# Attention and a mixture of experts on one Trainium2 core: the last sums loaded first, stored from another queue and shared with GpSimd; one batch's choice a call later; four fillers of each head behind a group of transposes

## The chip, the cores and the metric

The kernel runs on one core of a Trainium2 chip, in one launch. A core has a matrix engine (TensorE; in the profile PE, its weight loads PEld), VectorE (DVE), ScalarE (ACT) and GpSimd (POOL), each with an instruction stream of its own, and SyncE (SP), which here only issues transfers. Transfers run on 16 DMA engines; each issuing engine has a queue. Work is held in SBUF (128 partitions), matmul results in PSUM, which has eight banks of 128 x 512 float32.

The metric is the device time of the launch in microseconds (us). The kernel before took 1003.43 us, the median of three runs (1003.37 to 1006.6).

## The reference

2048 tokens of width E = 128, float32 throughout. Causal attention with H = 16 heads of D = 64, a residual, then a mixture of 8 experts (two of them per token, hidden width F = 352) beside a shared expert, and a residual:

```python
x = x + attention(layernorm(x))          # qkv with bias, causal softmax(q k / 8) v, out projection with bias
z = layernorm(x)
shared = (silu(z @ sg.T) * (z @ su.T)) @ sd.T
probs = softmax(z @ gate_w.T)             # 8 experts
topw, topi = top_k(probs, 2);  topw = topw / (topw.sum(-1) + 1e-20)
for e in 8 experts:                       # comb[t, e]: weight of expert e for token t, 0 where not chosen
    routed += (silu(z @ gw[e].T) * (z @ uw[e].T)) @ dw[e].T * comb[:, e]
x = x + shared + routed
```

## The kernel before, in words

**Attention.** Heads are handled in eight pairs j = 0..7 ("head" below means a pair; one takes about 100 us). A head runs through eight steps, each a pair m of token blocks of 128 (256 queries), in the order `turns = [2, 7, 0, 6, 1, 5, 3, 4]` (L393). Per step: scores of q and k (`score_units`, L438, `sc` in PSUM), scaled, masked and with their row maxima on VectorE (L449, L453), exponentials on ScalarE (L470), the probabilities turned, multiplied with v (`times_v`, L570, `av`), divided by their sums (`divide`, L591, the tile `aT`, of which there is one) and projected back to width 128 (`project`, L597, `po`), which is added to the residual `xr` (L598). So a probability row must be turned between exponential and value product. For m below 4 TensorE does it: `turn` (L538) transposes into a PSUM tile `tr` and ScalarE copies that to a tile `pT` (L541). For m of 4 and above ("near" in the code) the leading part is turned by VectorE's 32 x 32 transposes and a trip through device memory (`turn_slabs` stores to `staged`, `load_turned` loads it back as `turned`); only the last two or four blocks are turned by TensorE, by `turn_last`, which copies them to the tile `tail`.

**Fillers.** While head j runs, the queries, keys and values of head j + 1 are made by twelve short units: `qk_unit` (L361: one matmul of 128 x 512 into `pq`; keys are then copied by ScalarE at L373, queries by VectorE) and `v_unit` (L378: four matmuls into `pv`, copied by ScalarE at L385). They stand in the queue `fill`, one taken per group of a step. In the loop over steps and groups (L681 to L758) a step whose m is below 4 takes its filler at the start of a group, ahead of the group's transposes (L715 to L717), and a near step after the value products, ahead of `turn_last` of the step two later (L739 to L748).

**Order.** TensorE and VectorE work in the order in which the code writes their instructions (L630). ScalarE's and GpSimd's instructions are ordered by a scheduler. Six PSUM banks go round under the tag "r" for `sc`, `tr`, `pq`, `pv`, `po` and the rest; two hold `av`. A new tile takes the place of the one that was given out longest ago, so a matmul that writes `sc` may wait for the copy that empties a `tr`.

**Choice of experts.** When a pair of steps in the last head is finished, `route_units` makes the choice of experts for its four token blocks: normalised rows, their transposes, logits (`pr`, L260), the best expert (`best1`, six small VectorE operations and an exponential), the second best (`best2`), ranks by a matmul with a triangular matrix (`rk`, L301), then scatters of the rows to `zbuf` (L328). It returns a list of units, `None` meaning that a call does nothing; `route_on` (called up to three times in a group) takes the next one. For batches 0 and 1 the list is statistics, normed, None, turn, None, logits, None, best1, best2, None, None, ranks.

**Experts.** Rows come back sorted by expert in 39 blocks of 128, each goes through gate, up and down products, and GpSimd scatters the result to `ybuf` (L991). Each token has two rows there. The shared expert is done in four groups of 512 tokens; the group `late` (2) comes after all the experts' blocks, and its result `py` is added to `xr` at L811.

**End.** A loop over the four groups of 512 tokens in order 0, 1, 2, 3 loads the group's two rows per token (`yt`, 0.52 MB, L1026, on SyncE's queue), adds them to `xr` with two VectorE operations (L1028), and stores the group (L1031, on SyncE's queue too). As the scheduler put it before, SyncE issues three loads, the store of group 0, the fourth load and the other stores.

Of the kernel before, what the change touches and what calls it, by code (L numbers as in the profile page):

```python
# [10 lines left out]
F32 = mybir.dt.float32  # L11
# [5 lines left out]
P = 128  # L17
# [6 lines left out]
def attention_then_moe(  # L24
# [32 lines left out]
    nc = tc.nc  # L57

    _, S, E = x.shape
# [5 lines left out]
    NG = NT // 4  # L65
# [5 lines left out]
    out2 = out.rearrange("b (t p) e -> p (b t) e", p=P)  # L71
# [6 lines left out]
    xr = const.tile([P, NT, E], F32, name="xr")  # L78
# [4 lines left out]
    def load_wq(j, engine):  # L83
        wq_of[j] = norm.tile([P, 3, 2, D], F32, tag="wq", name=f"wq_{j}", bufs=3)
        engine.dma_start(wq_of[j], qkv_w[:, :, 2 * j : 2 * j + 2, :])
# [7 lines left out]
    with nc.allow_non_contiguous_dma(reason="1024 numbers"):  # L93
# [16 lines left out]
        fill=MASKED,  # L110
# [6 lines left out]
    for e in range(NE):  # L117
# [9 lines left out]
        fill=0.0,  # L127
# [86 lines left out]
    def route_units(blocks, number):  # L214
        n, k0 = len(blocks), blocks[0]
# [119 lines left out]

        turns = [lambda t0=t0: turn_row(t0) for t0 in range(0, n, 4)]
        chosen = [logits, None, best1, best2, ranks]
        if number < 2:
            chosen[4:4] = [None, None]
        if number == len(batches) - 1:  # L340
            return [statistics, normed, *turns, logits, best1, best2, ranks]
# [12 lines left out]
    def qkv_units(j):  # L354
        kT = pool.tile([P, S], F32, tag="kT", name=f"kT_{j}")
        qT = [None] * NG
        vt = pool.tile([P, NT, P], F32, tag="vt", name=f"vt_{j}")

        def qk_unit(s, n):
            pq = psp.tile([P, 512], F32, tag="r", name=f"pq_{j}_{s}_{n}")  # L360
            nc.tensor.matmul(  # L361
                pq,
                wq_of[j][:, s, :, :],
                xnT[:, ts(n, 512)],
                start=True,
                stop=True,
            )
            bias = bqk[:, s, j : j + 1]
            if s == 0:
                qT[n] = pool.tile([P, 512], F32, tag=f"qT{n}", name=f"qT_{j}_{n}", bufs=1)  # L370
                nc.vector.tensor_scalar_add(qT[n], pq, bias)  # L371
            else:
                nc.scalar.activation(kT[:, ts(n, 512)], pq, AF.Identity, bias=bias)  # L373

        def v_unit(g):
            pv = psp.tile([P, 4, P], F32, tag="r", name=f"pv_{j}_{g}")
            for t in range(4):
                nc.tensor.matmul(  # L378
                    pv[:, t, :],
                    xnT[:, ts(4 * g + t, P)],  # L380
                    wq_of[j][:, 2, :, :],
                    start=True,
                    stop=True,
                )
            nc.scalar.copy(vt[:, ts(g, 4), :], pv)  # L385

        q, k = ([lambda s=s, n=n: qk_unit(s, n) for n in range(NG)] for s in range(2))
        return (kT, qT, vt), q, k, [lambda g=g: v_unit(g) for g in range(NG)]
# [10 lines left out]
    def by_slabs(m):  # L399

        return (2 * m) // 4 * 4 if 2 * m >= NT // 2 else 0
# [130 lines left out]
    def turn(j, m, b, dst):  # L532

        tr = psp.tile([P, 2, 256], F32, tag="r", name=f"tr_{j}_{m}_{b}")
        q0 = 1 if b == 2 * m + 1 else 0
        for h in range(2):
            for q in range(q0, 2):
                nc.tensor.transpose(  # L538
                    tr[:, h, ts(q, P)], rows_of[j, m][q][:, h, ts(b, P)], ident
                )  # L540
        nc.scalar.copy(dst[:, :, q0 * P :], tr[:, :, q0 * P :])  # L541

    def turn_last(j, m):

        tail_of[j, m] = pool.tile([P, 4, 2, 256], F32, tag="tail", name=f"tail_{j}_{m}", bufs=1)
        for b in range(by_slabs(m), 2 * m + 2):
            turn(j, m, b, tail_of[j, m][:, b - by_slabs(m)])
# [41 lines left out]
    def divide(j, m):  # L589
        aT = pool.tile([P, 256], F32, tag="aT", name=f"aT_{j}_{m}", bufs=1)  # L590
        nc.vector.tensor_mul(aT, av_of[j, m], inb_of[j, m])  # L591
        return aT
# [28 lines left out]
    steps = [(j, m) for j in range(NP) for m in turns]  # L621
    qkv = {0: qkv_units(0)}

    def scores_of(n):
        if n >= len(steps):
            return deque()
        j, m = steps[n]
        return deque(score_units(j, m, *qkv[j][0][:2]))
# [14 lines left out]
    fill, later = deque(), deque()  # L643
# [20 lines left out]
    def route_on():  # L664

        for units in routes:
            u = units.popleft()
            if u:
                u()
        routes[:] = [units for units in routes if units]  # L670
# [10 lines left out]
    for n, (j, m) in enumerate(steps):  # L681
        at = n % NM
        if at == 0 and j + 1 < NP:
            qkv[j + 1] = qkv_units(j + 1)


            _, q, k, v = qkv[j + 1]
            fill.extend([*k, *v, q[3]])
            later.extend([q[1], q[0], q[2]])
            if j + 2 < NP:  # L690
                load_wq(j + 2, nc.sync)
        if at == 0 and j == NP - 1:
            load_shared()
        if at == 5 and later:
            assert not fill
            fill.extend(later)
            later.clear()
        if at == 6 and j + 1 < NP:
            assert not fill
        near = by_slabs(m)  # L700
        coming = scores_of(n + (4 if near else 2))
        if n == 0:
            coming.extend(scores_of(3))

        if near:
            groups = [list(range(near, 2 * m + 2))]
            groups += [list(range(k, k + near // 2)) for k in range(0, near, near // 2)]

            runs = [3, 3, len(coming) - 6] if n > 1 else [0, 3, 3]
        else:  # L710
            groups = [list(range(k, min(k + 3, 2 * m + 2))) for k in range(0, 2 * m + 2, 3)]
            half = len(coming) // 2 if n else 6
            runs = {1: [len(coming)], 2: [2 * (half // 2), half], 3: [0, half, half]}[len(groups)]
        for k, group in enumerate(groups):
            for _ in range(1 if n else 3):  # L715
                if fill and not near:
                    fill.popleft()()  # L717
            if n == 2:
                turn_slabs(2, age=False)
            turn_slabs(1)  # L720
            now = [turned(j, m, b) for b in group]
            if k == 0:
                spread(j, m)
            if ending is not None:
                finish(*ending)
                ending = None
            if n >= len(steps) - 2 and (n < len(steps) - 1 or k < 2):
                route_on()
            ready, last = (last + now, []) if near else (last, now)
            for t in ready:  # L730
                jt, mt, b = t[:3]
                times_v(*t, qkv[jt][0][2])
                if b == (by_slabs(mt) or 2 * mt + 2) - 1:
                    assert ending is None
                    ending = (jt, mt, divide(jt, mt))
            if n < len(steps) - 2:
                route_on()

            for _ in range(1 if n > 1 or k == 2 else 2):  # L739
                if fill and near:  # L740
                    fill.popleft()()
            if n < 2 and k == 1 - n:
                turn_slabs(2, age=False)
            turn_slabs(1, age=False, due=True)
            if n >= len(steps) - 2:
                route_on()
            if near and k == 0 and n + 2 < len(steps):
                turn_last(*steps[n + 2])  # L748
            if n == 0 and k == 0:
                turn_last(*steps[1])  # L750
                load_turned(*steps[1])
            if near and k == 1 and n + 2 < len(steps):
                load_turned(*steps[n + 2])
            for _ in range(runs[k] if k < len(groups) - 1 else len(coming)):
                if coming:
                    coming.popleft()()
            if len(steps) - 4 <= n < len(steps) - 2:
                route_on()  # L758
# [8 lines left out]
    ffn = ctx.enter_context(tc.tile_pool(name="ffn", bufs=2, reuse_waits="tile"))  # L767
# [47 lines left out]
    late = turns[-1] // 2  # L815
# [25 lines left out]
    number, started, which, mine, left, real = (tabs[:, k, :] for k in range(6))  # L841
# [179 lines left out]


    yb = ybuf.rearrange("(t p s) e -> p t (s e)", p=P, s=2)
    for g in range(NG):
        yt = ffn.tile([P, 4, 2 * E], F32, tag="yt", name=f"yt_{g}", bufs=NG)
        nc.sync.dma_start(yt, yb[:, ts(g, 4), :])  # L1026
        for k in range(2):
            nc.vector.tensor_add(  # L1028
                xr[:, ts(g, 4), :], xr[:, ts(g, 4), :], yt[:, :, k * E : (k + 1) * E]
            )  # L1030
        nc.sync.dma_start(out2[:, ts(g, 4), :], xr[:, ts(g, 4), :])  # L1031


# [53 lines left out]
```

## Time and profile before

| What | us |
|---|---|
| median of three runs | 1003.43 (1003.37 to 1006.6) |
| the profiled execution's own time | 1008.16 |
| its span, first to last instruction | 1006.30 |
| TensorE busy (share of the span) | 943.7 (94%) |
| VectorE busy | 749.7 (75%) |
| ScalarE busy | 540.9 (54%) |
| GpSimd busy | 204.9 (20%) |
| scores L438, TensorE | 298.0 in 1280 matmuls, mean 552 ns |
| value products L570, TensorE | 237.9 in 1920 matmuls |
| transposes L538, TensorE | 121.4 in 896 |
| fillers L361, TensorE | 71.3 in 128 |
| exponentials L470, ScalarE | 306.2 in 256 |
| scatters L991, GpSimd | 38.3 in 39 |

The span is what the trace shows; the execution's own time has 1.86 us more around it. The profile is of one execution, and the times are of others. Busy time is time in which an engine runs an instruction; its idle time is put down to the instruction that ended it. Where the prediction shows a line such as `431.66 0.83 ACT L541 COPY tail<-tr ... x2`, the columns are the start in us, the length of the stretch in us, the engine, the line of the code, the operation, the tile written and the tiles read, the shapes, and how many instructions of the kind follow on each other; in square brackets stands the idle time just ahead and what ended it. "PEclk" is the clock that TensorE was granted, 1.00 being full speed. An issue of a transfer is listed under its queue (SPq for SyncE's).

### The profile page before, as it was taken

What the parts mean: (1) busy time and instruction counts of PE and PEld (TensorE: products, weight loads), DVE (VectorE), ACT (ScalarE), POOL (GpSimd) and SP (SyncE); (2) the same over time, 40 slices, a digit from 0 to 9 for tenths busy, and PEclk for the clock granted to TensorE, in tenths of its full rate; (3) what the DMA queues carried; (4) which work ended last, traced back from release to release, by engine and by line L of the source; (5) the groups of instructions that cost most, each with busy time, mean ns of one, the idle gap of its engine ahead of it and who ended that gap; (6) DMA issues with size and microseconds to landing.
All of it is one profiled execution on the core that took longest, in us unless ns stands there. A gap on an engine that the chain in (4) does not pass through costs nothing. (4 is left out here: it accounts for less than half of the span.)

```text
span 1006.3 us, 18409 instructions
## 1 busy us (share of the span) xinstructions
PE 943.7 (94%) x5930; PEld 567.9 (56%) x5930; DVE 749.7 (75%) x2359; ACT 540.9 (54%) x1017; POOL 204.9 (20%) x393
## 2 busy tenths in 40 slices
PE   4998899999999999999999999999999898989996
PEld 1464555565556555655565556555655455657774
DVE  3786788778877877787778777877788886755554
ACT  4573556555655565556555655565466553425552
POOL 2040111111111111111111111111211103634441
PEclk9998999999999999999999999999999997999998
DMA  9568648864896488748874887588648864723104
GB/s 329 173 203 288 198 149 267 261 220 155 261 276 206 155 260 265 216 157 261 270 210 157 260 266 210 164 256 270 209 150 274 268 193 146 216 61 85 40 24 132
DMA packets 112670, 205.31 MB, mean 204 GB/s; under 512 B 16864, under 2 KB 104258, under 8 KB 107456
## 3 DMA queue, kind: packets, MB, share of 16 engines
q1 hardware_dynamic: 102816, 190.65, 59.4%
q0 software_dynamic: 8032, 13.22, 5.5%
q8 instruction: 48, 0.79, 0.3%
q10 hardware_dynamic: 1728, 0.27, 0.2%
q14 instruction: 46, 0.38, 0.1%
HBM read 105.10 MB, written 99.35 MB: 203 GB/s over the span
## 5 line engine op out<-in xcount | busy, mean ns | idle before, releaser
L470 ACT ACTIVATE row<-row,neg 128x1920 f32<-128x1920 f32 (+15 forms) x256 | 306.2, 1202 | 198.7 <-DVE neg L467 87.3
L438 PE MATMUL sc<-kT,qT 64*128 64x512 f32 (+3 forms) x1280 | 298.0, 552 | 11.3 <-ACT tail L541 5.2
L449 DVE TENSOR_SCALAR_CACHE_REDUCE row<-sc 128x512 f32<-128x512 f32 x384 | 243.3, 685 | 76.4 <-PE sc L438 65.8
L438 PEld LDWEIGHTS sc<-kT,qT 64*128 64x128 f32 x1280 | 123.9, 186 | 152.5 <-issue 83.6
L512 DVE STREAM_TRANSPOSE row<-row 128x1024 f32<-128x1024 f32 (+1 forms) x128 | 190.3, 1491 | 5.1 <-ACT row L470 5.1
L570 PE MATMUL av<-turned,vt 128*64 128x256 f32 x1280 | 158.3, 395 | 2.1 <-DMA turned<-stage 2.1
L453 DVE CUSTOM_DVE_ANT_0 row<-sc,mask 128x384 f32<-128x384 f32 (+3 forms) x256 | 114.9, 486 | 18.2 <-PE sc L438 17.6
L538 PE MATMUL tr<-ident,row 128*128 128x128 f32 x896 | 121.4, 281 | 6.5 <-DVE row L449 2.1
L538 PEld LDWEIGHTS tr<-ident,row 128*128 128x128 f32 x896 | 102.2, 144 | 41.1 <-issue 19.4
L570 PEld LDWEIGHTS av<-turned,vt 128*64 128x64 f32 x1280 | 88.5, 140 | 64.9 <-issue 23.5
L501 POOL DMA_DIRECT2D invd<-inv x60 | 43.1, 718 | 392.1 <-DVE inv L499 285.1
L541 ACT COPY pT<-tr 128x512 f32<-128x512 f32 (+1 forms) x160 | 78.6, 553 | 77.6 <-PE tr L538 77.2
L583 POOL DMA_DIRECT2D inb<-invd x120 | 71.6, 602 | 187.8 <-DMA invd<-inv 112.7
L570 PE MATMUL av<-pT,vt 128*64 128x256 f32 (+1 forms) x640 | 79.6, 371 | 6.3 <-ACT pT L541 5.9
L361 PE MATMUL pq<-xnT,wq 128*128 128x512 f32 x128 | 71.3, 647 | 0.1
L570 PEld LDWEIGHTS av<-pT,vt 128*64 128x64 f32 x640 | 38.5, 136 | 46.9 <-ACT pT L541 18.8
L541 ACT COPY tail<-tr 128x512 f32<-128x512 f32 x96 | 43.9, 520 | 15.1 <-PE tr L538 15.1
L991 POOL DMA_INDIRECT ybuf<-yo,to x39 | 38.3, 982 | 61.3 <-ACT yo L990 61.3
L371 DVE TENSOR_SCALAR qT<-pq,bqk 128x512 f32<-128x512 f32 x32 | 23.9, 747 | 34.6 <-PE pq L361 34.6
L470 ACT ACTIVATION_READ_ACCUMULATOR row<-row,neg 128x1 f32 x256 | 49.6, 194 | 0.0
L597 PE MATMUL po<-wo,aT 128*128 128x128 f32 x256 | 43.7, 294 | 5.7 <-DVE rest L280 2.5
L597 PEld LDWEIGHTS po<-wo,aT 128*128 128x128 f32 x256 | 34.0, 193 | 22.9 <-DVE row L449 16.3
(170 smaller groups left out, 894.8 us busy)
## 6 DMA issues: line engine op xcount, KB each, us to landing
stage<-row SPq DMA_DIRECT2D x256, 192.0 KB, 3.7
turned<-stage SPq DMA_DIRECT2D x16, 3072.0 KB, 11.1
stage<-row SPq DMA_DIRECT2D x256, 128.0 KB, 2.7
turned<-stage SPq DMA_DIRECT2D x16, 2048.0 KB, 8.7
zbuf<-zeros SPq DMA_DIRECT2D x8, 1056.0 KB, 11.4
inb<-invd POOLq DMA_DIRECT2D x120, 64.0 KB, 3.2
zs<-zbuf SPq DMA_DIRECT2D x39, 66.0 KB, 1.8
yt<-ybuf SPq DMA_DIRECT2D x4, 512.0 KB, 4.2
```

Source lines behind the costliest of these rows:

```text
L361: nc.tensor.matmul(pq, wq_of[j][:, s, :, :], xnT[:, ts(n, 512)], start=True, stop=True,)
L438: nc.tensor.matmul(sc[:, :cw], qT[i // 4][hd, ts(i % 4, P)], keys, start=True, stop=True)
L449: nc.vector.tensor_scalar(dst, src, SCALE, None, ALU.mult, ALU.max, accum_out=mh)
L453: nc.vector.tensor_tensor_reduce(out=rows[:, h, c0 : c0 + cw], in0=scs[h][:, :cw], in1=mask[:, 512 - cw : 512], scale=SCALE, scalar=-F32_M ...
L470: nc.scalar.activation(row, row, AF.Exp, bias=neg[:, h : h + 1], accum_out=sums[:, h : h + 1])
L501: small_dma(j, m)(invd_of[j, m].rearrange("n (a i) -> a n i", a=4), inv,)
L512: nc.vector.transpose(row, row)
L538: nc.tensor.transpose(tr[:, h, ts(q, P)], rows_of[j, m][q][:, h, ts(b, P)], ident)
L541: nc.scalar.copy(dst[:, :, q0 * P :], tr[:, :, q0 * P :])
L570: nc.tensor.matmul(av_of[j, m][hd, q0 * P :], vt[:, b, hd], pT[:, h], start=(b == near), stop=(b == (near or 2 * m + 2) - 1),)
L583: small_dma(j, m)(inb[h * D : (h + 1) * D, :].rearrange("d (q p) -> d q p", q=2), row.partition_broadcast(D),)
L597: nc.tensor.matmul(po[:, q, :], aT[:, ts(q, P)], wo[:, j, :], start=True, stop=True)
```

## The change

Three parts, and nothing is computed differently.

1. **Fillers and `turn_last`.** In the first step of a head (m = 2, two groups; not in the very first step of the run) the second group takes its filler behind the group's transposes and ahead of the value products, where it took it ahead of the transposes. In near steps, `turn_last` of the step two later comes ahead of the first group's filler, where it came behind it (for all steps but the run's second, where it stays). Other steps are as they were.
2. **Choice of the first batch.** One more None ahead of `best1` and one fewer behind `best2`: `best1` and `best2` come one call later, and ranks at the same call. The second batch keeps its list.
3. **End.** All four loads are written ahead of the sums, in the order 0, 1, 3, 2; the second of them, group 1, is added by GpSimd; the stores go out on ScalarE's queue.

```diff
         chosen = [logits, None, best1, best2, ranks]
-        if number < 2:
+        if number == 0:
+            chosen = [logits, None, None, best1, best2, None, ranks]
+        if number == 1:
             chosen[4:4] = [None, None]
...
             for _ in range(1 if n else 3):
-                if fill and not near:
+
+                if fill and not near and (at or not k or not n):
                     fill.popleft()()
...
             if n >= len(steps) - 2 and (n < len(steps) - 1 or k < 2):
                 route_on()
+            if n and not at and k and fill:
+                fill.popleft()()
             ready, last = (last + now, []) if near else (last, now)
...
             if n < len(steps) - 2:
                 route_on()
+            if n > 1 and near and k == 0 and n + 2 < len(steps):
+                turn_last(*steps[n + 2])
 
             for _ in range(1 if n > 1 or k == 2 else 2):
                 if fill and near:
...
-            if near and k == 0 and n + 2 < len(steps):
+            if n == 1 and k == 0:
                 turn_last(*steps[n + 2])
...
     yb = ybuf.rearrange("(t p s) e -> p t (s e)", p=P, s=2)
-    for g in range(NG):
-        yt = ffn.tile([P, 4, 2 * E], F32, tag="yt", name=f"yt_{g}", bufs=NG)
-        nc.sync.dma_start(yt, yb[:, ts(g, 4), :])
+    by_group = [g for g in range(NG) if g != late] + [late]
+    yts = {}
+    for g in by_group:
+        yts[g] = ffn.tile([P, 4, 2 * E], F32, tag="yt", name=f"yt_{g}", bufs=NG)
+        nc.sync.dma_start(yts[g], yb[:, ts(g, 4), :])
+    for g in by_group:
+        engine = nc.gpsimd if g == by_group[1] else nc.vector
         for k in range(2):
-            nc.vector.tensor_add(
-                xr[:, ts(g, 4), :], xr[:, ts(g, 4), :], yt[:, :, k * E : (k + 1) * E]
+            engine.tensor_add(
+                xr[:, ts(g, 4), :], xr[:, ts(g, 4), :], yts[g][:, :, k * E : (k + 1) * E]
             )
-        nc.sync.dma_start(out2[:, ts(g, 4), :], xr[:, ts(g, 4), :])
+        nc.scalar.dma_start(out2[:, ts(g, 4), :], xr[:, ts(g, 4), :])
```

How this falls out in the instruction streams: TensorE's and VectorE's are as written, ScalarE's copies follow their matmuls. In heads 1 to 6 four fillers per head end up behind a group of transposes: the second keys unit in m = 2, the third keys unit in m = 7, a values unit in m = 6 and a queries unit in m = 5; in head 0 only the one in m = 5. There, in heads 1 to 6, the first copy of the tail of m = 4 also comes ahead of the exponentials of m = 7 on ScalarE, where it stood behind them. The streams of SyncE and GpSimd are the same up to the end; there SyncE issues four loads in a row and ScalarE, behind all its other work, the four stores in the order 0, 1, 3, 2.

## The prediction

> **What bounds the kernel now.** I read the busy times by stretch first, then TensorE's order of time over one head, then ScalarE and VectorE at the same instants, and last the queues of the end.
>
> ```profile
> core 0: us, PE busy (x) PEld busy (x) DVE busy (x) ACT busy (x) POOL busy (x), PEclk, DMA share, GB/s
> 270.00:390.00 120.00, 116.87 (x769) 67.58 (x769) 94.91 (x279) 71.21 (x130) 20.21 (x40) 1.00 0.74 223
> ...
> 820.00:832.20 12.20, 9.94 (x70) 6.05 (x68) 11.51 (x43) 8.05 (x19) 0.00 (x0) 1.00 0.58 142
> 832.20:845.90 13.70, 12.91 (x57) 8.91 (x58) 7.60 (x47) 2.72 (x8) 2.99 (x3) 0.50 0.60 206
> ```
>
> In the middle of the run TensorE is busy 97% of the time; VectorE has a fifth free, ScalarE two fifths. So time can only be won from TensorE's gaps. They recur with each head, 100.24 us apart (the wait at 332.04 us in head 2 comes again at 432.27 in head 3). Around 832 us the granted clock is 0.50 for 13.7 us; I come back to that.
>
> ```profile
> 427.36 1.13 PE L361 MATMUL pq<-xnT,wq 128*128 128x512 f32 x2
> 428.32 0.82 PE L538 MATMUL tr<-ident,row 128*128 128x128 f32 x6
> 429.07 2.59 PE L438 MATMUL sc<-kT,qT 64*128 64x512 f32 x8
> 432.27 1.40 PE L438 MATMUL sc<-kT,qT 64*128 64x512 f32 x4 [0.62 <-ACT tail L541]
> 433.60 0.71 PE L597 MATMUL po<-wo,aT 128*128 128x128 f32 x4
> ```
>
> ```profile
> 429.38 1.15 ACT L470 ACTIVATE row<-row,neg 128x1024 f32<-128x1024 f32 x1 [3.02 <-DVE neg L467]
> ...
> 431.57 0.18 ACT L470 ACTIVATION_READ_ACCUMULATOR row<-row,neg 128x1 f32 x1
> 431.66 0.83 ACT L541 COPY tail<-tr 128x512 f32<-128x512 f32 x2
> ```
>
> This is the largest gap that a moved filler stands at. The filler pq comes ahead of the transposes tr, so tr ends only at 429.1; ScalarE, idle for 3.02 us until 429.38, then has two exponentials first and copies tr out of PSUM at 431.66. The scores sc need those PSUM tiles: 12 matmuls from 429.07 to 433.60 are 4.53 us, where the undisturbed group at 389.55 takes 2.78.
>
> ```profile
> 829.38 1.06 PE L260 MATMUL pr<-gwT,xnT 128*128 128x8 f32 x8
> 832.99 1.19 PE L597 MATMUL po<-wo,aT 128*128 128x128 f32 x4 [2.55 <-DVE rest L280]
> 834.11 3.68 PE L570 MATMUL av<-turned,vt 128*64 128x256 f32 x16
> ```
>
> The projection po waits 2.55 us, really for aT, which VectorE makes at 832.44 behind six small operations of the first batch's choice (831.27 to 832.44).
>
> ```profile
> 991.47 1.49 SPq L1026 DMA_DIRECT2D yt<-ybuf  x3
> 996.73 0.38 SPq L1031 DMA_DIRECT2D out_dram<-xr  x1
> 997.15 0.51 SPq L1026 DMA_DIRECT2D yt<-ybuf  x1
> 998.58 4.57 SPq L1031 DMA_DIRECT2D out_dram<-xr  x3
> ```
>
> ```profile
> 997.87 2.02 DVE L1028 TENSOR_TENSOR xr<-xr,yt 128x512 f32<-128x512 f32 x3
> 1001.33 1.42 DVE L1028 TENSOR_TENSOR xr<-xr,yt 128x512 f32<-128x512 f32 x2 [1.45 <-DMA yt<-ybuf]
> ```
>
> The fourth load stands behind a store that waits for sums, so it starts 5.7 us after the first and the last sums end at 1002.75.
>
> **Fillers and turn_last.** Nothing is added: the same matmuls and copies in another order, no DMA among them; SyncE's and GpSimd's queues keep their order here. Per head four fillers move from ahead of a group of transposes to behind it.
> (a) First key/query filler of step m=2. In head 3, tr comes 0.86 us earlier (pq takes 372.23 to 373.09), but the next av waits for a copy that ScalarE makes at 375.28, after two exponentials of 1.80 and 1.79 us. The filler was before that wait and is still before it, so the 0.98 us wait at 375.91 stays. Only the copy of pq (0.71 us) no longer stands ahead of three pT copies; the score pair at 377.31 took 0.78 us against 0.53 for the same pair at 413.96. I take 0.1, with 0 and 0.25 as bounds.
> (b) Filler of m=7: no gap there. Behind tr, its kT copy (0.69 us) comes last and would be done at about 383.45; the score that reuses its tile begins at 384.4. Nothing, with 0.9 us of cover.
> (c) Filler of m=6 (four value products): the copy comes after four tail copies (1.84 us from about 404.0), done at about 406.5; its user begins at 407.35. Nothing, cover 0.85 us.
> (d) Filler of m=5, the gap shown: tr ends at about 428.1, ScalarE is idle, and in the changed order the first tail copy is ahead of the exponentials. Left behind them is the second, of 128x256 (0.38 us, row at 360.00): 431.66 + 0.38 = 432.04. Only the last score product waits for it: two passes, 0.53 + 0.43, to 433.06 instead of 433.60. That is 0.54. Bounds: 0 if another copy takes the place, 1.75 (4.53 - 2.78) if the wait vanished.
> In head 0 ScalarE's order is unchanged; I give it nothing. Heads 1 to 6: 6 x 0.64 = 3.8 us. It stays won if nothing later holds absolute time: the next loads of turned rows land well ahead (issued 410.64, median 11.1 us to landing, used 434.24), and VectorE waits for TensorE at 437.28 (1.91 us).
>
> **First batch's choice.** Six VectorE operations, 1.09 us, go from ahead of aT to behind it. po starts 1.1 us sooner. Next, rk waits for the choice itself, which ends when it did (834.3). At full clock TensorE reaches rk at 834.4, so no wait; then it reaches the second batch's rk earlier, and that waits for a VectorE chain which stays where it was: VectorE works without a break from 822 to 836.5. So at full clock 0.2 of the 1.1 is left; at half clock, where VectorE idles 3.57 us at 840.07, the whole 1.1. Bounds 0 and 1.1.
> The row with the half clock: 16 av matmuls take 3.61 us at 834.11 and 1.88 at 434.24. From po to the second rk (832.99 to 846.50) half rate costs about 6.3 us, some 5.5 after the VectorE chain. The Trainium skill (TensorE: Matmul & The Clock Gate, HAM oscillation) says that idle gaps over some 3.4 us throttle the array. Here the gap was 2.55 us and the clock fell all the same, so the row decides; by the rule no throttle stood here to be lost.
>
> **End.** All four loads issue from 991.47, 0.55 apart. The engines moved 382 GB/s while three loads were queued (993.5 to 997.0), so 2.10 MB from about 993.2 end at 998.7; with the first group's store (0.26 MB, issued about 996.8) mixed in, 999.4. VectorE: group 0 to 996.65, py to 997.95, group 3 to 999.2, the late group from 999.5 to 1000.9, against 1002.75: 1.85 us. GpSimd adds group 1. The trace has no 128x512 add on it: 128x128 takes 0.45 (paced 0.415), memsets grow from 0.19 to 0.53 for the same step in size. Between 1.2 and 1.8 each; I take 1.5, the add being the nearer row, so 996.5 + 3.0 = 999.5, before the late group. It stands behind the last scatter (ended 990.32), and nothing is behind it but group 3's and the late group's stores, which follow group 1's in ScalarE's queue; that queue's last activation ended at 993.5. Stores take 2.4 us to land, as before. Less 0.15 for stores that overlap: 1.7 us. Bounds 0.3 (adds of 1.8 and a late start) and 2.2.
>
> **Sum.** The profiled execution took 1008.16 us, span 1006.30 with 1.86 around it: less 3.8, 1.1 and 1.7 makes 1001.6. The runs' median is 1003.43, 4.73 lower, about what the half clock costs, so I take the median as free of it: 1003.43 - 3.8 - 0.2 - 1.7 = 997.7. About 0.5% (5 us, below 998.4 or above 1008.4) is what a measurement of this kernel can tell from no change.
>
> **Rivals.**
> 1. Half clock avoided. If the runs behind the median carry it, and po's earlier start keeps the clock, the choice is worth 1.1 + 4: about 992.8. For it: the profiled run. Against: 1.5 us of idle is left, after 1.06 us of tiny pr matmuls. Chance 0.12.
> 2. GpSimd and VectorE exclude each other in the sums. Each add of VectorE there reads two SBUF tiles, as GpSimd's do. If they take turns, from 996.65 on 3.0 us of GpSimd and four VectorE adds of 0.63 stand one after the other: 1002.2, a gain of 0.6 instead of 1.7, so 998.8. No row of the trace has both at once, so it is open. The Trainium skill (SBUF — State Buffer, SBUF: two separate sides) states such a lock, held for the whole instruction. Chance 0.22.
> 3. The gap at (d) moves on to another wait of the same head; fillers give 0 to 0.1 a head: about 1001.2. For it: ScalarE's exponentials end when they did. Chance 0.17.
> 4. Slower. The copy of the moved filler is now last in ScalarE's line at (b) and (c), and a score product reuses its tile. If ScalarE or the semaphores run 0.9 us later than I read, TensorE waits there by up to a copy (0.69 and 0.59) in six heads, 7.7 us, and (d)'s gain goes the same way: 1003.43 - 0.2 - 1.7 + 7.7 = 1009.2. It decides from 0.9 us of lateness. Against: ScalarE stands idle for 4 us after each. Chance 0.08.
>
> **How the numbers follow.** The forecast, 997.7, has 0.41, and alone would range from 996 to 999.5. The range 993.0 to 1002.2 takes in rivals 2 and 3 and the better part of 1. Faster by over 0.5%: two thirds of the forecast (0.28), rival 1 (0.12), and a third of rival 2 and a little of 3 (0.10): 0.50. Slower by over 0.5%: most of rival 4, with a chance stall in it, 0.07. The rest, 0.43, is within 0.5%.
>
> **What would show it.** (a) to (c): the 0.98 us wait of av stays, and no new wait of sc for kT or vt appears. (d): the sc group falls from 4.53 to about 4.0 us and the head's period from 100.24 to about 99.6. Choice: po's wait of 2.55 falls to about 1.45; a wait at the second rk at full clock. End: four yt issues in a row, GpSimd adds of 1.2 to 1.8 us, last VectorE add ending some 9.4 us after the first load's issue instead of 11.3. A period that doesn't move, or adds on VectorE stretched to over 1 us, would make me wrong.

## The result, and the profile after

The changed kernel takes 999.94 us, the median of 20 runs (997.99 to 1003.98), against 1004.08 us for the kernel before in 20 runs beside them (1001.55 to 1008.70): ratio 0.9960, 95% interval 0.9948 to 0.9973, so 2.7 to 5.2 us faster. The profiled execution took 1000.75 us with a span of 998.8; before it was 1008.16 and 1006.3.

So the forecast of 997.7 had the direction and was 2.2 us low. Behind that lies one term of the wrong sign: the end of the kernel, which was to gain 1.7 us, lost 2.1.

The heads first. TensorE's order of time over the same place of head 3 as before (start, length, engine, line, operation, tiles; in brackets the idle time ahead and what ended it):

```profile
425.90 0.87 PE L540 MATMUL tr<-ident,row 128*128 128x128 f32 x6
426.61 1.02 PE L363 MATMUL pq<-xnT,wq 128*128 128x512 f32 x2
427.56 2.84 PE L440 MATMUL sc<-kT,qT 64*128 64x512 f32 x10
430.60 1.12 PE L440 MATMUL sc<-kT,qT 64*128 64x512 f32 x2 [0.20 <-ACT tail L543]
431.65 0.71 PE L599 MATMUL po<-wo,aT 128*128 128x128 f32 x4
```

ScalarE at the same time:

```profile
426.64 0.59 ACT L543 COPY tail<-tr 128x512 f32<-128x512 f32 x1 [1.75 <-PE tr L540]
427.92 1.15 ACT L472 ACTIVATE row<-row,neg 128x1024 f32<-128x1024 f32 x1 [0.69 <-DVE neg L469]
...
429.07 1.13 ACT L472 ACTIVATE row<-row,neg 128x1024 f32<-128x1024 f32 x1
...
430.20 0.35 ACT L543 COPY tail<-tr 128x256 f32<-128x256 f32 x1
```

The transposes now come ahead of the filler. The first tail copy is made in ScalarE's idle time; the second still stands behind both exponentials, and only the last score pair waits for it. The twelve score products take 4.09 us (427.56 to 431.65) where they took 4.53. From the last step of head 0 to that of head 6 the changed kernel gains 3.67 us on the one before: in each of heads 1 to 6 0.13 by the projection of m=2, 0.04 to 0.05 more at that of m=0 and 0.48 to 0.49 more at that of m=1, which are the next ones behind the moved fillers (the expectations below call the last two "after m=7" and "after m=6"); once, in head 3, 0.25 is lost at the projection of m=0.

Head 7, where the first batch's choice is made:

```profile
827.49 0.68 PE L599 MATMUL po<-wo,aT 128*128 128x128 f32 x4 [1.53 <-DVE best L265]
828.10 3.61 PE L572 MATMUL av<-turned,vt 128*64 128x256 f32 x16
831.64 0.41 PE L301 MATMUL rk<-hot,below 128*128 128x40 f32 x2
```

The wait is 1.53 us instead of 2.55, and the 16 av matmuls behind it still take 3.61 us: the clock is halved here too (PEclk in the rows below, the third number from the end), but from 828.2 for 3.4 us where it was 13.7.

```profile
core 0: us, PE busy (x) PEld busy (x) DVE busy (x) ACT busy (x) POOL busy (x), PEclk, DMA share, GB/s
824.80:828.20 3.40, 1.87 (x16) 1.59 (x16) 3.23 (x16) 2.34 (x6) 0.00 (x0) 1.00 0.86 220
828.20:831.60 3.40, 3.40 (x16) 1.59 (x16) 3.00 (x20) 1.20 (x3) 0.00 (x0) 0.50 0.34 73
831.60:845.30 13.70, 12.51 (x100) 9.15 (x98) 10.21 (x65) 6.31 (x15) 7.89 (x8) 1.00 0.60 209
```

That difference is worth 4.46 us in this pair of profiles (the gain grows from 5.50 to 9.96 us from the projection at 827.49 to the next); it returns below.

The end, in order of time (SPq and ACTq are the queues of SyncE and ScalarE):

```profile
981.91 2.04 SPq L1035 DMA_DIRECT2D yt<-ybuf  x4
...
985.85 1.42 DVE L1039 TENSOR_TENSOR xr<-xr,yt 128x512 f32<-128x512 f32 x2 [0.93 <-DMA yt<-ybuf]
987.28 3.12 POOL L1039 TENSOR_TENSOR xr<-xr,yt 128x512 f32<-128x512 f32 x2 [6.53 <-DMA yt<-ybuf]
987.30 5.38 ACTq L1042 DMA_DIRECT2D out_dram<-xr  x4
987.51 0.69 DVE L818 TENSOR_TENSOR xr<-xr,py 128x512 f32<-128x512 f32 x1 [0.24 <-PE py L811]
988.58 3.69 DVE L1039 TENSOR_TENSOR xr<-xr,yt 128x512 f32<-128x512 f32 x4 [0.39 <-DMA yt<-ybuf]
```

Four loads in a row, two adds by GpSimd, VectorE through at 992.27, the last store issued at 992.30 (to 992.68): as forecast in kind. But the span ends at 998.8. Counted from the end of the last scatter (990.32 before, 980.75 after) VectorE's last add ends 0.9 us sooner, at 11.52 instead of 12.43 us, and the span ends 2.1 us later, at 18.06 instead of 15.98. What fills the time is not in the busy rows. It is in the rows of the program's last line, which list the drains, instructions named DRAIN that every engine runs at the end of the program (first the kernel before, then the changed one; the three numbers are the shortest, the median and the longest in ns, then the first and last start):

```profile
L1082 POOLq DRAIN  x3: 45/107/8885, 989.0 to 1006.0; - x3
L1082 SPq DRAIN  x3: 7/7/7, 1005.4 to 1005.8; - x3
```

```profile
L1093 POOLq DRAIN  x3: 45/107/9423, 988.6 to 998.5; - x3
L1093 SPq DRAIN  x3: 7/7/7, 995.0 to 998.3; - x3
```

GpSimd's first drain starts at 989.0 and takes 8.9 us before, to 997.9, which is 7.6 us behind its last scatter; SyncE was there to see the last store landed only at 1005.5. In the changed kernel it starts at 988.6 and takes 9.4 us, to 998.0, 7.6 us behind the last add (987.28 + 3.12 = 990.40). SyncE is through at 995.1, and all engines wait for GpSimd 2.9 us longer.

### The profile page after: what moved, and what is told of

Read it like the earlier page. It is cut to its first block, busy times and chain, and to the rows that moved or that the text cites. A ratio compares the mean times of both kernels' runs of the same rounds, so it can differ in the third digit from the quotient of the medians.

```text
span 998.8 us, 18408 instructions
## 1 busy us (share of the span) xinstructions
PE 936.2 (94%) x5930; PEld 560.1 (56%) x5930; DVE 748.9 (75%) x2357; ACT 541.3 (54%) x1017; POOL 208.0 (21%) x395
## 5 line engine op out<-in xcount | busy, mean ns | idle before, releaser
L572 PE MATMUL av<-turned,vt 128*64 128x256 f32 x1280 | 155.4, 390 | 1.2 <-DMA turned<-stage 1.2
L540 PEld LDWEIGHTS tr<-ident,row 128*128 128x128 f32 x896 | 99.2, 142 | 35.3 <-DVE row L451 13.9
L363 PE MATMUL pq<-xnT,wq 128*128 128x512 f32 x128 | 69.3, 631 | 0.1
L572 PEld LDWEIGHTS av<-pT,vt 128*64 128x64 f32 x640 | 38.5, 136 | 50.5 <-issue 20.5
L967 DVE TENSOR_TENSOR hk<-sk,uk 128x352 f32<-128x352 f32 x39 | 20.3, 520 | 35.4 <-PE uk L963 35.4
```

The lines of the kernel that those rows point to most:

```text
L363: nc.tensor.matmul(pq, wq_of[j][:, s, :, :], xnT[:, ts(n, 512)], start=True, stop=True,)
L540: nc.tensor.transpose(tr[:, h, ts(q, P)], rows_of[j, m][q][:, h, ts(b, P)], ident)
L572: nc.tensor.matmul(av_of[j, m][hd, q0 * P :], vt[:, b, hd], pT[:, h], start=(b == near), stop=(b == (near or 2 * m + 2) - 1),)
```

## The experiments

Their ratios are to the kernel before, run beside them on the same chip: 1003.82 us for the first four, 1020.48 for the second four, on another chip (the "second chip" below), 1004.16 for the last four. "After the last scatter" is from the end of GpSimd's last scatter to the end of the span, in the profile of each. "Gain" is how much earlier than in the first profile of the kernel before a projection comes, step by step, so that what differs ahead of the first head drops out.

### Group 1 added by VectorE (all_vector), and the changed end alone (end_only)

```diff
-        engine = nc.gpsimd if g == by_group[1] else nc.vector
+        engine = nc.vector
```

> The changed kernel with one edit: group 1's two adds are made by VectorE again. Theory (GpSimd's drain is the new end): in the changed kernel GpSimd's last add ends at 990.39 us and its drain at 998.00, 7.6 us later, while the last store has landed by 994.6 and SyncE is through at 995.1. Without the adds GpSimd's last work is the last scatter, its drain is over about 7.6 us after that and hidden; the end then waits for the last store. VectorE makes eight adds and py back to back, last one ending at about the same distance from the last scatter (11.4 us, 11.5 in the changed kernel). From the end of the last scatter to the end of the span: about 15.1 us instead of 18.07, so about 2.9 us faster than the changed kernel and some 7 us (0.7%) faster than before. Rival (stores on ScalarE's queue or the four loads in a row are what lengthens the end): still 17.5 us or more after the last scatter, no faster than the changed kernel. Rival (GpSimd's help is worth something): VectorE's last add ends 1 us or more later than 11.5 after the last scatter.

Measured: 995.56 us (994.57 to 998.95), ratio 0.9916 (0.9893 to 0.9939). After the last scatter 14.43 us.

```profile
984.67 2.05 DVE L1039 TENSOR_TENSOR xr<-xr,yt 128x512 f32<-128x512 f32 x3 [0.80 <-DMA yt<-ybuf]
986.64 0.68 DVE L818 TENSOR_TENSOR xr<-xr,py 128x512 f32<-128x512 f32 x1
987.24 3.34 DVE L1039 TENSOR_TENSOR xr<-xr,yt 128x512 f32<-128x512 f32 x5
```

```profile
L1093 POOLq DRAIN  x3: 45/107/8887, 978.4 to 993.9; - x3
```

VectorE does all nine operations without a pause and is through 10.87 us after the last scatter, 0.65 sooner than with GpSimd's help; the drain lies at 978.4 to 987.3, under the sums. The drain theory holds, and the end is even shorter than expected of it (15.1). The theories that blamed the stores' queue or the order of the loads fall.

The counterpart is the kernel before with the changes of the end only (the diff's last hunk).

```diff
+        engine = nc.gpsimd if g == by_group[1] else nc.vector
...
-        nc.sync.dma_start(out2[:, ts(g, 4), :], xr[:, ts(g, 4), :])
+        nc.scalar.dma_start(out2[:, ts(g, 4), :], xr[:, ts(g, 4), :])
```

> The kernel before with the changed end alone (loads first, stores on ScalarE's queue, group 1 by GpSimd). Theory (GpSimd's drain): from the last scatter's end to the end of the span 18.1 us instead of 15.98, so about 2.1 us slower than before (ratio about 1.002). Rival (the end gains, as the prediction had it, and the profile of the changed kernel was an unlucky one): 14.3 us after the last scatter, 1.7 us faster (ratio 0.998).

Measured: 1006.64 us (1003.46 to 1009.02), ratio 1.0018 (1.0003 to 1.0033), slower by 0.3 to 3.3 us; 18.04 us after the last scatter. The loss is the end's own.

### A small copy by GpSimd (small_last)

To part the drain from the adds: all_vector with one copy of 128 x 1 by GpSimd behind the last load.

```diff
+    small_copy = ffn.tile([P, 1], F32, name="small_copy", bufs=1)
+    nc.gpsimd.tensor_copy(small_copy, yts[late][:, 0, :1])
     for g in by_group:
```

> The kernel that has group 1 added by VectorE, with one small copy (128 x 1) by GpSimd behind the last load. It leaves nothing out and adds one number per partition. Theory (GpSimd's drain takes a fixed 7.6 us from its last instruction and sets the end): the copy runs about 10 us after the last scatter's end, the drain ends some 7.6 us behind it, and from the last scatter to the end of the span it is about 18.3 us instead of 14.4; 3.5 to 4 us slower than without the copy. Rival (the adds and what VectorE loses to them cost the 3 us, not the drain): the copy of 128 numbers costs nothing, 14.4 to 14.8 us after the last scatter.

Measured: after the last scatter 18.17 us; the three other kernels of this call, with the same end but for the copy, have 14.57 to 14.59. Ratio 0.9969 (0.9948 to 0.9991), against 0.9955 (0.9935 to 0.9974) and 0.9959 (0.9941 to 0.9976) for two of them that lack other parts of the change, so the medians alone would not decide it; the trace does. GpSimd's work, then its drain:

```profile
1006.56 0.41 POOL L1037 COPY small_copy<-yt 128x1 f32<-128x1 f32 x1 [9.34 <-DMA yt<-ybuf]
```

```profile
L1095 POOLq DRAIN  x3: 45/107/8035, 1006.5 to 1015.1; - x3
```

The copy ends at 1006.97, the drain at 1006.5 + 8.0 = 1014.6, 7.6 us behind it. A copy of 0.41 us costs 3.6 us. It is the place of GpSimd's last instruction that counts, not its size.

### The stores' queue (sync_stores)

```diff
-        nc.scalar.dma_start(out2[:, ts(g, 4), :], xr[:, ts(g, 4), :])
+        nc.sync.dma_start(out2[:, ts(g, 4), :], xr[:, ts(g, 4), :])
```

> The kernel with group 1 added by VectorE, with the stores on SyncE's queue as before the change. Theory (ScalarE's queue is worth nothing, the four loads ahead of the stores are what helps): from the last scatter to the end of the span 14.4 to 14.7 us, the same time. Rival (the queue matters): 1 us or more later, as the first store of SyncE would wait behind something.

Measured (all_vector with this edit): 14.54 us after the last scatter; 995.68 us (995.02 to 996.45), ratio 0.9917 (0.9890 to 0.9944). The queue is worth nothing once the loads are written first. Of the end's three parts only the order of the loads gains: 15.98 to about 14.5 us (fillers_only and choice_only, whose end is the old one, have 16.06 and 15.63).

### The fillers alone (fillers_only), and one place of the four (one_place)

The first is the kernel before with the four hunks of the loop only.

```diff
-                if fill and not near:
+                if fill and not near and (at or not k or not n):
...
+            if n and not at and k and fill:
+                fill.popleft()()
...
+            if n > 1 and near and k == 0 and n + 2 < len(steps):
+                turn_last(*steps[n + 2])
```

> The kernel before with the fillers' and the transposes' places alone. Theory (the gain of each head stays won): head by head the projection comes 0.13 us earlier after m=2, 0.04 after m=7 and 0.49 after m=6, 0.6 to 0.66 per head, about 3.9 us by the last step of head 6 counting 0.26 of head 0; all of it is still there at the last scatter, if the clock's half stretches are equal; ratio about 0.996. Rival (the gain is taken back in head 7 or by the experts, which wait for transfers): under 2 us left at the first experts' block, ratio 0.998 or more.

Measured: 999.11 us (998.18 to 1001.06), ratio 0.9952 (0.9933 to 0.9971). The gain grows from 0.87 us at the end of head 0 to 4.78 at the end of head 6: 3.91 us, 0.65 a head. Nothing is taken back behind it: the gain is 5.72 us at the fifth projection of head 7 (that of m=1, ahead of which the choice stands; the "third" of the expectations below), and 10.02 at the last scatter, the clock's share with it. The theory holds.

The second is all_vector with only the place in m=5 changed.

```diff
-            if n and not at and k and fill:
-                fill.popleft()()
...
-            if n > 1 and near and k == 0 and n + 2 < len(steps):
+            if at == 5 and k == 0 and n + 2 < len(steps):
                 turn_last(*steps[n + 2])
```

(The other conditions are those of the kernel before; its own `turn_last` call is skipped at at == 5.)

> The kernel that has group 1 added by VectorE, with one of the four places of a head alone: turn_last ahead of the filler in m=5, the other three as before the change. Theory (the place in m=5 makes nearly all of the fillers' gain): 0.49 us per head at the projection after m=6, nothing after m=2 and m=7, 2.9 us by the last step of head 6. Rival (the four act together, for example through the order of PSUM banks): under 0.3 or over 0.6 us per head.

Measured: 0.48 to 0.49 us per head at the projection of m=1, nothing at those of m=2 and m=0; 2.9 us in six heads, of which 0.45 is lost once, in head 5 between the projections of m=2 and m=7, where other heads show no such loss. Ratio 0.9959 (0.9941 to 0.9976). This place is three quarters of the fillers' gain, on its own.

### Both tail copies ahead of the exponentials (tail_first, tail_first_2)

What is left at that place is the second copy. ScalarE is idle for 0.69 us ahead of the exponentials (the 427.92 line above), enough for it. An ordering edge with no wait is put from the exponentials of block 7 to the last copy, on top of all_vector; the other engines' orders stay the same.

```diff
+        if m == 4:
+            for later in exps_of.get((j, 7), []):
+                tc.add_manual_dep(
+                    later.ins,
+                    ins.ins.name,
+                    mybir.DependencyInfo(
+                        mybir.DependencyClass.NoSync, mybir.DependencyReason.DATA
+                    ),
+                    reason="tail first",
+                )
```

(`exps_of` keeps the exponentials of each block, `ins` is the last copy of `turn_last`.)

> The kernel that has group 1 added by VectorE; in m=5 both copies of the tail of m=4 now come ahead of the two exponentials of block 7 on ScalarE, in every head (there the first copy was ahead already, in heads 1 to 6). Theory (what is left at this place, 4.09 us for 12 score products instead of 2.78, is the second copy alone): ScalarE is idle for 0.69 us ahead of the exponentials, the copy takes 0.38, so the group falls to about 2.8 to 3.0 us, 1.1 to 1.3 us per head in heads 1 to 6 and up to 1.75 in head 0, 6.6 to 9 us in all if it stays won; ratio 0.983 to 0.986. Rival (the gap moves on to VectorE's row maxima, which free the other banks): at most 0.3 us a head, ratio 0.989 to 0.992.

Measured on the second chip: 1005.43 us (1004.26 to 1008.24), ratio 0.9855 (0.9833 to 0.9876). TensorE, then ScalarE, at the same place of head 3:

```profile
423.06 0.88 PE L542 MATMUL tr<-ident,row 128*128 128x128 f32 x6
423.78 1.02 PE L363 MATMUL pq<-xnT,wq 128*128 128x512 f32 x2
424.73 2.85 PE L440 MATMUL sc<-kT,qT 64*128 64x512 f32 x12
427.51 0.71 PE L611 MATMUL po<-wo,aT 128*128 128x128 f32 x4
```

```profile
423.81 0.86 ACT L545 COPY tail<-tr 128x512 f32<-128x512 f32 x2 [1.75 <-PE tr L542]
425.09 1.15 ACT L472 ACTIVATE row<-row,neg 128x1024 f32<-128x1024 f32 x1 [0.41 <-DVE neg L469]
```

The copies fit into the idle time, the exponentials wait only for VectorE as before, and the twelve products take 2.78 us (424.73 to 427.51): the length of the undisturbed group. The gap did not move on.

> Both copies of the tail ahead of the exponentials once more, against the kernel without it on the same chip: 1.31 us per head at the projection after m=6 in heads 1 to 6 and 1.9 in head 0, 9.8 us in all; theory (it stays won): 8 us or more below that kernel's median, ratio about 0.982 to before. Rival (head 7's transfers take it back): under 5 us below.

Measured: 987.85 us (985.96 to 988.04), ratio 0.9832 (0.9809 to 0.9856), beside 996.92 for all_vector on the same chip: 9.1 us less. The gain per head is 1.99 us where all_vector has 0.66, so 1.33 from the second copy. That is 16.3 us less than the kernel before, where the change itself gained 4.1.

### The choice (choice_only, no_choice, all_vector_2, no_choice_2)

```diff
-        if number < 2:
+        if number == 0:
+            chosen = [logits, None, None, best1, best2, None, ranks]
+        if number == 1:
             chosen[4:4] = [None, None]
```

> The kernel before with the first batch's choice one call later alone. Theory A (at full clock next to nothing, as the prediction had it): the wait of the first projection behind that batch falls from 2.55 to about 1.5 us, the next wait at the second batch's ranks takes most of it back, median change 0 to -1 us, and half clock of 13.65 us there is as frequent as before. Theory B (the shorter wait keeps the clock): the stretch at half clock near 830 us stays at 3.4 us or falls away in the profile, granted clock 0.985 to 0.99 in nearly all runs, 3 to 5.5 us faster (ratio 0.995 to 0.997).

Measured, with this hunk alone on the kernel before: 1001.63 us (999.33 to 1005.56), ratio 0.9978 (0.9960 to 0.9996). In its profile the clock is not halved anywhere near 830 us, po waits 1.53 us, and the second batch's rk waits 0.82 us for VectorE, as the prediction had it for full clock. The granted clock has a mean of 0.988 in 12 runs, beside 0.986 in 24 of the kernel before. That spoke for theory B, without proving it.

> The kernel that has group 1 added by VectorE, with the first batch's choice put back where it was. Timed beside nothing else of the change: fillers and end as in that kernel (995.56 us median, ratio 0.9916). Theory A (the choice moves 1.0 us of waiting, no clock): 1.0 us slower at the third projection of head 7 and up to the experts, median 996 to 997, ratio 0.992 to 0.994. Theory B (the choice's shorter wait also keeps the clock): a stretch at half clock of 7 us or more near 828 us in the profile, and 3 us or more slower, ratio 0.995 or more.

```diff
-        if number == 0:
-            chosen = [logits, None, None, best1, best2, None, ranks]
-        if number == 1:
+        if number < 2:
             chosen[4:4] = [None, None]
```

Measured (all_vector with this edit): 1016.19 us (1011.51 to 1018.11), ratio 0.9955 (0.9935 to 0.9974). Inconclusive: on this chip head 7 loses some 15 us between the projections of m=5 and m=3 (26.9 us from one to the next, 11.7 in all_vector), behind the choice, which hides what the choice is worth. Both were therefore run once more together. The 17.7 us that the last expectation of this section names are VectorE's wait for TensorE's av; TensorE in turn waits for ScalarE there (7.18 us ahead of 849.85), not for a load of turned rows.

> The changed kernel with group 1 added by VectorE once more, so that the next three can be compared on one chip. From the last scatter to the end of the span 14.4 to 14.6 us as before; ratio 0.99 to 0.994.

> The same with the first batch's choice put back. On the chip of its first run head 7 waited 17.7 us for a load of turned rows behind the choice, so nothing could be read of it there. Theory A (the choice moves 1.0 us of waiting, no clock): 0.8 to 1.1 us more at the third projection of head 7 and 0 to 1.1 us in the median against the kernel with the choice moved. Theory B (the shorter wait also keeps the clock): 3 us or more in the median, and longer stretches at half clock near 830 us.

Measured: all_vector 996.92 us (996.01 to 998.80), ratio 0.9930 (0.9908 to 0.9952), 14.53 us after the last scatter; without the choice 998.10 (996.50 to 999.27), ratio 0.9939 (0.9918 to 0.9960). 1.2 us between the medians, but the runs of the two overlap, so that the medians alone don't tell it from nothing; the traces must. Both profiles have 3.4 us of half clock there (from 829.0 and from 827.6). The gain that the choice makes at the fifth projection is 1.01 us, and 1.06 us is seen at the next: nothing is given back. How that comes is shown by fillers_only (choice not moved), TensorE and then VectorE, where the first batch's ranks are used:

```profile
827.27 0.78 PE L597 MATMUL po<-wo,aT 128*128 128x128 f32 x4 [2.54 <-DVE rest L280]
827.98 3.49 PE L570 MATMUL av<-turned,vt 128*64 128x256 f32 x16
...
836.96 0.39 PE L301 MATMUL rk<-hot,below 128*128 128x40 f32 x2 [0.50 <-DVE hot L283]
```

```profile
832.71 0.19 DVE L318 TENSOR_TENSOR at<-rk,base 128x32 f32<-128x32 f32 x1 [1.94 <-PE rk L309]
```

and by all_vector (choice moved):

```profile
826.53 0.68 PE L599 MATMUL po<-wo,aT 128*128 128x128 f32 x4 [1.53 <-DVE best L265]
827.14 3.16 PE L572 MATMUL av<-turned,vt 128*64 128x256 f32 x16
...
836.21 0.39 PE L301 MATMUL rk<-hot,below 128*128 128x40 f32 x2 [0.50 <-DVE hot L283]
```

```profile
831.97 0.19 DVE L318 TENSOR_TENSOR at<-rk,base 128x32 f32<-128x32 f32 x1 [0.82 <-PE rk L309]
```

The half-clock stretch slows the av matmuls so that VectorE waits for the ranks, 1.94 us in the one and 0.82 in the other. With that slack the whole 1.1 us passes through VectorE's chain, and the second rk waits 0.50 in both.

Theory A holds for the price, about 1 us. Theory B falls for the changed kernel: in the seven profiles with the fillers' change (the second chip left out) the stretch at half clock near 830 us is 3.4 us long, in five with the choice moved and in two without. It begins within 1.3 us of the end of po's wait, which is 1.53 us in the five, so the shorter wait does not keep the clock up. On the second chip, too, the stretch is 3.4 us in no_choice, and none, 3.4 and 10.2 us in the three with the choice moved. Nor is the 4.46 us of the result the choice's: fillers_only gains 4.48 at the same place. Without the fillers' change there are three profiles: 13.7 and 10.2 us with the choice where it was, none with it moved. There theory B may hold, and choice_only's 2.2 us would then have some clock in them; three profiles don't settle it. What makes the stretch long or short stays open.

## Why the prediction was right and where it was wrong

- **Fillers (3.8 us): right, in mechanism and size.** 3.67 us in the profile of the changed kernel, 3.91 with the fillers alone. At (a) 0.13 was measured for 0.1: the 0.98 us wait of av is still there, and five pT copies now run in a row. At (b) and (c) no new wait appeared; 0.04 was gained there where nothing was forecast, and which of the two makes it was not tried. At (d) 0.49 for 0.54, for the reason given; tail_first showed that the second copy was all that was left of the 1.75 us bound. Rivals 3 and 4 fall.
- **First batch's choice (0.2 us): mechanism right, size wrong.** The term taken was that of full clock; 1.0 us was measured. The step that failed is "I take the median as free of it": of the ten profiles that are not from the second chip, nine had at least 3.4 us of half clock behind po, and the slack that this gives to VectorE is what the prediction's own upper bound (1.1) stands for. In the one profile at full clock the 0.82 us wait at the second rk, which the prediction foresaw, is there. Rival 1, the clock kept by an earlier po, is not borne out in the changed kernel.
- **End (1.7 us gained): wrong in sign, 2.1 us lost.** The step that failed is "It stands behind the last scatter (ended 990.32), and nothing is behind it but group 3's and the late group's stores": GpSimd's drain is behind it, 7.6 us, and the end waits for that. The drain stood in the trace of before, with 7.6 us of cover (997.9 to 1005.5). In parts: the loads first gain 1.55 us (15.98 to 14.43), GpSimd's adds delay the last VectorE add by 0.65 and, by the drain, the end by a further 3.0. The estimate for an add was good: 1.26 us alone and 1.77 beside VectorE, for 1.5. The help could not have gained much in any case: rid of group 1, VectorE waits for group 3's load (0.39 us at 988.58), and in all_vector, doing all nine operations, it is through 10.87 us after the last scatter, where the prediction's 1000.9 with GpSimd's help lies at 10.6.
- **Rival 2, the shared port: its mechanism was there, at a part of its price.** VectorE's fourth add of the changed kernel took 1.63 us (989.31 to 990.94) for its usual 0.69, and ended 0.55 behind GpSimd's second add; that one had started while a VectorE add ran and took 1.77 us for 1.26. VectorE's add of py, one of whose inputs is in PSUM, took its 0.69 beside GpSimd's first add. The Trainium skill (SBUF — State Buffer, SBUF: two separate sides) says that the pair of ports is locked for whole instructions, and against VectorE only where that reads two SBUF inputs or runs in a mode that uses two ports: the trace agrees in all three cases. The add stretched to over 1 us, which the prediction named as a sign of being wrong, was thus there once: 0.94 us longer, and 0.65 at the last add against the kernel without GpSimd's help, for the 1.1 of the rival, since only one pair of adds met on each side. The adds in one view (the three numbers are the shortest, the median and the longest in ns):

```profile
L1039 DVE TENSOR_TENSOR xr<-xr,yt x6: 679/692/1632, 985.9 to 991.6; 128x512 f32<-128x512 f32 x6
L1039 POOL TENSOR_TENSOR xr<-xr,yt x2: 1263/1518/1773, 987.3 to 988.6; 128x512 f32<-128x512 f32 x2
```

- **The sum.** With the terms as the traces have them, -3.7 - 1.0 + 2.1 = -2.6 us; measured -4.1, with -2.7 to -5.2 as interval. The three parts run alone have medians of -4.7, -2.2 and +2.8, which add up to that -4.1; each is 0.7 to 1.2 us more than its trace shows, and within its own interval. What is over is not assigned: single runs of the changed kernel lie 6 us apart, with granted clocks of 0.982 to 0.990, and the long stretch of half clock behind po may have become rarer. That the forecast came within 2.2 us is partly luck: the end was 3.8 us worse than its term, the choice 0.8 better, and some 1.5 us of the gain has no term. The change is 0.4%, so that faster by over 0.5%, to which the prediction gave the highest chance (0.50), did not come; by 20 runs of each the gain can still be told from none.

## What to carry to other kernels

A kernel is over when the last engine has drained, so an engine that is idle near the end is not free to use: look in the trace at what follows its last instruction, and count that as part of the price. Here GpSimd's last work must end at least 7.6 us before SyncE has seen the last store land. Where a moved group of transposes gains something because its copies now come ahead of a long activation, look whether all of the copies do; the scheduler's order of one engine can be corrected with an ordering edge that adds no wait, and here that was worth twice the whole change.

## What the runs showed of the hardware

- GpSimd's first drain ended 7.60 to 7.62 us behind its last instruction in all fourteen profiles, whether that was a scatter, an add of 1.77 us or a copy of 0.41 us. VectorE's drain at the end of the changed kernel took 0.73 us, ScalarE's 0.15. What GpSimd does in that time the trace does not show.
- Stretches at half clock came in multiples of 3.41 us (3.4 to 20.5), but for those that the end of the span cuts off. In head 7 of the changed kernel one began 0.7 us after the end of a wait of TensorE of only 1.53 us. The Trainium skill (TensorE: Matmul & The Clock Gate, HAM oscillation) puts the gap that throttles at over some 3.4 us; the traces differ here, and they decide.
- On the second chip the kernel before took 1020.48 us. In the four profiles from there head 7 stalls behind m=5; in that of no_choice ScalarE stands still for 2.28, 2.98 and 8.49 us (ahead of 845.25, 848.82 and 859.43), ended by something outside what the profile shows, and TensorE waits for it. The other ten profiles do not show it, and its cause is open.
